# Four graph-attention layers: VectorE reads the row factors G from SBUF instead of from a copy in PSUM

## The chip, the core and the metric

The kernel runs on one core of one Trainium2 chip. The metric is the device time of one execution in microseconds (us). The kernel before took 2712.34 us, the median of three runs (2709.53 to 2713.56).

Engine names as in the profile: PE is TensorE (PEld its weight loads), DVE is VectorE, ACT is ScalarE, POOL is GpSimd, SP is the engine that issues most transfers.

## The reference, cut to what matters

The input `x` has 16 graphs of 1024 nodes with 256 features, all with one 1024 x 1024 adjacency matrix. Four layers follow one another. Each normalises the rows, projects them, forms attention weights over the neighbours, sums the projected rows with them, and adds the result to `x`:

```python
h = jnp.maximum(_layernorm(x, axis=-1), 0.0)
x = x + layer(h, adj, W, a)

# layer, per head (layers 0 and 2 have four heads of 64, layers 1 and 3 one head of 256)
q = h @ W
e = q @ a_src [:, None] + q @ a_dst [None, :]
e = where(e >= 0, e, slope * e)
attn = softmax(where(adj > 0, e, -inf), axis=-1)
out = elu(attn @ q)            # relu in the last layer
```

## The kernel before

The exponential of a leaky sum is the larger of two products, so a tile of unnormalised weights needs no exponential of its own: up to factors that cancel or that are moved into the projected rows, it is `max(G[i], r[j]) * mask[j, i]`, with `G` a row (one value for each target node `i`) and `r` a column (one for each neighbour `j`). VectorE makes such a tile of 128 neighbours by 1024 target nodes in one instruction, TensorE multiplies it with the projected rows, and a column of ones in them gives the denominator.

There are 16 x 4 = 64 steps (graph, layer); half have four heads, half have one. A head has eight weight tiles, so there are 32 x 4 x 8 + 32 x 8 = 1280 in all. The steps of four graphs are interleaved, and the preparation of a step is spread over the aggregation of the steps ahead of it by lists of places (`agenda`).

Preparation of a step, and the pools in which its results lie:

```python
xpool = ...(name="xpool", bufs=STREAMS)                    # STREAMS = 4
ps_g = ...(name="ps_g", bufs=2, space=PSUM)                # G: two banks each
ps_acc = ...(name="ps_acc", bufs=2, space=PSUM)
ps_p = ...(name="ps_p", bufs=2, space=PSUM)

def stats(half):
    for c in range(half * HALF, (half + 1) * HALF):
        nc.vector.bn_stats(bn[:, c, :], xs[b][:, c, :])    # L191
    if half == 1:                                          # L198 to L207
        nc.gpsimd.tensor_tensor(dev, m0, m1, op=ALU.subtract)
        ...                                                # ten short operations on 128 x 8
        nc.gpsimd.tensor_tensor(rstd, rstd, neghalf, op=ALU.pow)        # L204
        ...
        nc.gpsimd.tensor_scalar(shift, shift, -0.5, None, op0=ALU.mult)

def normalise(half):
    for q in range(HALF):
        nc.scalar.activation(xn[:, q, :], xs[b][:, c, :], AF.Identity,  # L213
                             bias=st["shift"][:, c:c + 1], scale=st["rstd"][:, c:c + 1])

def transpose(half, k):
    pt = ps_p.tile([P, HALF, P], F32, name="pp")
    for q in range(HALF):
        nc.tensor.transpose(pt[:, q, :], st["xn", half][:, q, k * P:(k + 1) * P], ident)  # L221
    nc.scalar.activation(st["hT", half][:, k, :], ..., AF.Relu)         # L222

def project(c):
    pw = ps_p.tile([P, F + 2 * H], F32, name="pp")
    ... nc.tensor.matmul(pw, ...)                                       # L233
    ... nc.scalar.activation(whx[:, c, ...], pw[...], ...)              # L235 to L242
    ... nc.gpsimd.tensor_tensor(whx[...], whx[...], ..., op=ALU.mult)   # L244, four heads only
```

`G` goes through device memory to be spread over the partitions. It lands in SBUF (`gs`); ScalarE copies it to PSUM (`g`), and VectorE reads it there:

```python
def fetch(n, h):
    gs = state[n]["gs", h] = work.tile([P, N], F32, name="gs", bufs=2)
    nc.sync.dma_start(out=gs, in_=state[n]["grow"][h]....partition_broadcast(P))

def broadcast(n, h):
    g = state[n]["g", h] = ps_g.tile([P, N], F32, name="g")
    nc.scalar.activation(g, state[n]["gs", h], AF.Copy)                 # L284

def weights(n, h, jc):
    w = state[n]["w", h, jc] = work.tile([P, N], F32, name="w", bufs=WBUFS)   # WBUFS = 18
    nc.vector.scalar_tensor_tensor(w, state[n]["g", h],                 # L289
                                   state[n]["rcol"][:, jc, h:h + 1],
                                   masks[...][:, jc, :], op0=ALU.max, op1=ALU.mult)
```

The mask is a uint8 tile in SBUF. Aggregation and the finish of a step, which runs during the next step:

```python
def aggregate(n, h, i0, per):
    acc = ps_acc.tile([P, per, D + 1], F32, name="acc")
    ... nc.tensor.matmul(acc[...], lhsT=st["w", h, jc][:, o:o + cols],  # L305
                         rhs=st["whx"][:, jc, h, :], start=(jc == 0), stop=(jc == C - 1))
    nc.scalar.activation(st["y"][:, i0:i0 + per, h, :], acc, AF.Copy)   # L309

# finish, in two halves of 128 x 1024
nc.vector.reciprocal(r, y[..., D])                                      # L326
nc.gpsimd.tensor_tensor(yh, yh, r..., op=ALU.mult)                      # L330
nc.gpsimd.tensor_scalar(e, yh, 0.0, -3.0e38, op0=ALU.min, op1=ALU.max)  # L335
nc.scalar.activation(e, e, AF.Exp)                                      # L339
nc.vector.scalar_tensor_tensor(e, e, -1.0, yh, op0=ALU.add, op1=ALU.max)# L345
nc.gpsimd.tensor_add(xh, xh, e)                                         # L346
# last layer, in place of the last four: x = max(y, 0) + x
nc.vector.scalar_tensor_tensor(xh, yh, 0.0, xh, op0=ALU.max, op1=ALU.add)     # L348
```

The order in which VectorE's tiles are emitted is made by `emit_tiles`: a head's copy is emitted when the tiles come within four of it, and the tiles run ahead of TensorE as far as the weight buffers go, which come free a head at a time.

Of the kernel before, what the change touches and what calls it, by code (L numbers as in the profile page):

```python
# [23 lines left out]
F32 = mybir.dt.float32  # L24
# [3 lines left out]
AF = mybir.ActivationFunctionType  # L28
ALU = mybir.AluOpType
AX = mybir.AxisListType  # L30
PSUM = bass.MemoryType.PSUM

P = 128
EPS = 1e-5
SHIFT = 60.0
STREAMS = 4
WBUFS = 18

# [17 lines left out]
def kernel(ctx: ExitStack, tc: tile.TileContext, x, adj, ws, avs, out):  # L58
    nc = tc.nc
    B, N, F = x.shape  # L60
    C = N // P
# [27 lines left out]
    prep = ctx.enter_context(tc.tile_pool(name="prep", bufs=2))  # L89
    small = ctx.enter_context(tc.tile_pool(name="small", bufs=4))  # L90
    work = ctx.enter_context(tc.tile_pool(name="work", bufs=2))
    ps_g = ctx.enter_context(tc.tile_pool(name="ps_g", bufs=2, space=PSUM))
    ps_acc = ctx.enter_context(tc.tile_pool(name="ps_acc", bufs=2, space=PSUM))
    dram = ctx.enter_context(tc.tile_pool(name="dram", bufs=4, space=bass.MemoryType.DRAM))
    ps_p = ctx.enter_context(tc.tile_pool(name="ps_p", bufs=2, space=PSUM))

    L = len(LAYERS)
    steps = order_of_steps(B, L)
# [1 line left out]
    state = [dict() for _ in steps]  # L100
# [48 lines left out]
    def mask_block(jc):  # L149
# [3 lines left out]
        def fetch_block():  # L153
            st["raw"] = work.tile([P, C, P], I32, name="w", bufs=WBUFS)
            nc.scalar.dma_start(out=st["raw"], in_=adj.rearrange("(c p) j -> p c j", p=P)[
                :, :, jc * P:(jc + 1) * P])

        def sign():
            st["sgn"] = work.tile([P, 2, C, P], BF16, name="w", bufs=WBUFS)
            nc.vector.tensor_scalar(st["sgn"][:, 0], st["raw"], -1.0, 1.0, op0=ALU.max,  # L160
                                    op1=ALU.min)
# [17 lines left out]
    def preparation(n):  # L179
# [90 lines left out]


        out += [factors, rows, lambda: fetch_heads(n + 1), lambda: None]
        return [(at, piece) for at, piece in zip(agenda_of[n], out, strict=True)]

    def fetch(n, h):

        gs = state[n]["gs", h] = work.tile([P, N], F32, name="gs", bufs=2)
        nc.sync.dma_start(out=gs, in_=state[n]["grow"][h].rearrange("c i -> (c i)")
                          .partition_broadcast(P))

    def broadcast(n, h):

        g = state[n]["g", h] = ps_g.tile([P, N], F32, name="g")
        nc.scalar.activation(g, state[n]["gs", h], AF.Copy)  # L284

    def weights(n, h, jc):

        w = state[n]["w", h, jc] = work.tile([P, N], F32, name="w", bufs=WBUFS)
        nc.vector.scalar_tensor_tensor(w, state[n]["g", h], state[n]["rcol"][:, jc, h:h + 1],  # L289
                                       masks[LAYERS[steps[n][1]][3]][:, jc, :],  # L290
                                       op0=ALU.max, op1=ALU.mult)

# [72 lines left out]
    def groups(n):  # L365
        if LAYERS[steps[n][1]][0] == 1:
# [3 lines left out]
    tiles = [(n, h, jc) for n, (b, l) in enumerate(steps) for h in range(LAYERS[l][0])  # L370
             for jc in range(C)]
    place = {t: i for i, t in enumerate(tiles)}
    done = {"tiles": 0, "g": 0, "gs": 0, "rows": 0, "free": 0, "prepared": 0}
    agenda = []

    def prepare(upto):

        while agenda and agenda[0][0] <= upto:
            _, n, piece, last = agenda.pop(0)
            piece()  # L380
            if last:
                done["prepared"] = n + 1
# [6 lines left out]
    def fetch_heads(below=0):  # L389

        done["rows"] = max(done["rows"], below)
        while done["gs"] < min(done["g"] + 2 * C, len(tiles)):
            n, h, _ = tiles[done["gs"]]
            if n >= done["rows"]:
                break
            fetch(n, h)
            done["gs"] += C

    def emit_tiles(upto, must=False):
        while done["tiles"] < min(upto, len(tiles)):  # L400
            i = done["tiles"]

            while done["g"] <= min(i + C // 2, len(tiles) - 1):
                n, h, _ = tiles[done["g"]]
                if n >= done["prepared"]:
                    if i < done["g"] or not must:
                        break
                    prepare(max(a[0] for a in agenda if a[1] == n))
                broadcast(n, h)
                done["g"] += C  # L410
                fetch_heads()
            if i >= done["g"]:
                return
            weights(*tiles[i])
            done["tiles"] += 1

    last, agenda_of = {}, []
    for n, (b, l) in enumerate(steps):

        free = 8 * (last[b % STREAMS] + 1) + (8 if l == 0 else 5) if b % STREAMS in last else -99  # L420
# [17 lines left out]
    with tc.manual_schedule():  # L438
# [38 lines left out]
        planned = 2  # L477
        prepare(-2)
        emit_tiles(C, must=True)
        prepare(-1)  # L480
        for i in range(1, STREAMS):
# [7 lines left out]
        for n in range(len(steps)):  # L489
            for k, (h, i0, per) in enumerate(groups(n)):  # L490
                while planned < len(steps) and agenda_of[planned][0] <= 8 * n + k:
                    plan(planned)
                    planned += 1
                emit_tiles(place[n, h, C - 1] + 1, must=True)
                aggregate(n, h, i0, per)
                if i0 + per == C:
                    done["free"] = place[n, h, C - 1] + 1
                while ending and ending[0][0] <= k:
                    ending.pop(0)[1]()
                if 8 * n + k in later:  # L500
                    later[8 * n + k]()
                prepare(8 * n + k)
                ahead = 6 if per > 1 else 3
                emit_tiles(min(done["tiles"] + ahead, done["free"] + WBUFS))
            for _, piece in ending:
                piece()
            ending = finish(n)
# [35 lines left out]
```

## Time and profile before

| what | value |
|---|---|
| time, median of three | 2712.34 us |
| span of the profiled execution | 2711.9 us |
| mean granted TensorE clock | 0.984 |
| TensorE matmul busy | 2567.2 us, 95% |
| VectorE busy | 1900.3 us, 70% |
| ScalarE busy | 1229.6 us, 45% |
| GpSimd busy | 992.3 us, 37% |
| weight tiles on VectorE (L289) | 1280, mean 1273 ns |
| copies of G on ScalarE (L284) | 160, mean 1018 ns, 162.3 us |
| transfers, all queues | 130.12 MB, mean 48 GB/s |

The busy line of the page gives each engine's busy time, its share of the span, and its instructions. The chain that ended last is followed back from the last instruction: each piece is put down to what released it. The groups list instructions of one line with their tiles (out<-in), shape and count, then the busy time, the mean of one, and the idle time just before them with what ended it. In the waits, a line "PE acc L305 <- DVE w L289" is idle time of TensorE that VectorE's writing of w ended. The windows give each engine's busy time in a stretch of the span, and the timeline lists single instructions with start and length.

### The profile page before, as it was taken

How to read it: one execution, taken by the hardware profiler on the slowest of the kernel's cores; microseconds unless marked ns; L12 is line 12 of the kernel's file. 1: busy time of each engine (PE TensorE's matmuls, PEld its weight loads, DVE VectorE, ACT ScalarE, POOL GpSimd, SP SyncE). 2: the span in 40 equal slices, each digit the busy share in tenths (PEclk: the TensorE clock that was granted, in tenths of full speed). 3: DMA queues.
4: the chain of work that ended last, by engine and by line, in shares of the span. 5: the costliest groups of instructions: out<-in, count | busy, mean ns of one | idle time of the engine just before them, and what ended most of it. 6: DMA issues, size and time to landing. Idle time of an engine off the chain costs nothing.

```text
span 2711.9 us, 89498 instructions
## 1 busy us (share of the span) xinstructions
PE 2567.2 (95%) x40080; PEld 2269.2 (84%) x40080; DVE 1900.3 (70%) x2041; ACT 1229.6 (45%) x3337; POOL 992.3 (37%) x1242
## 2 busy tenths in 40 slices
PE   3799999999999999999999999999999999999998
PEld 2688888888888888888888888888888888788876
DVE  3796686477875688666876778748687567678752
ACT  3344445444354554544444454544435444444431
POOL 2133424423424534344242353442332443443321
PEclk9899999999999999999999999999999999999999
DMA  3211011012122011002201211101212110011111
GB/s 117 87 42 45 10 45 41 19 62 66 41 72 71 27 49 41 18 33 72 73 33 49 72 33 42 41 25 57 67 39 72 59 45 18 33 41 42 33 33 55
DMA packets 70846, 130.12 MB, mean 48 GB/s; under 512 B 6208, under 2 KB 49984, under 8 KB 70464
## 3 DMA queue, kind: packets, MB, share of 16 engines
q1 hardware_dynamic: 62144, 120.21, 13.5%
q8 instruction: 316, 5.18, 0.8%
q10 hardware_dynamic: 8320, 4.19, 0.6%
q14 instruction: 66, 0.54, 0.1%
HBM read 106.95 MB, written 17.43 MB: 46 GB/s over the span
## 4 chain that ended last, share of the span: by engine, by line
PE 81%; DVE 8%; ACT 4%; issue 3%; POOL 2%; DMA 1%; ACTq 0%; DVEq 0%; SPq 0%; POOLq 0%
PE acc L305 61%; PE pp L233 16%; DVE w L289 6%; PE pp L221 4%; ACT xn L213 1%; DVE bn L191 1%; DMA w<-in_adj 1%; ACT whx L235 1%; ACT g L284 1%; POOL rstd L204 0%; ACT e L339 0%; POOL y L330 0%; ACT whx L239 0%; PE pp L260 0%; DMA x<-in_x 0%
## 5 line engine op out<-in xcount | busy, mean ns | idle before, releaser
L305 PE MATMUL acc<-whx,w 128*64 128x65 f32 x36864 | 1951.0, 242 | 42.0 <-DVE w L289 28.6
L305 PEld LDWEIGHTS acc<-whx,w 128*64 128x64 f32 x36864 | 1766.8, 145 | 225.2 <-issue 70.4
L289 DVE SCALAR_TENSOR_TENSOR w<-g,rcol,mask 128x1024 f32<-128x1024 f32 x1280 | 1544.1, 1273 | 458.3 <-ACT g L284 412.3
L309 ACT ACTIVATE y<-acc 128x260 f32<-128x260 f32 (+1 forms) x512 | 196.8, 384 | 1085.8 <-PE acc L305 1085.0
L233 PE MATMUL pp<-wx,hT 128*128 128x258 f32 (+1 forms) x2048 | 513.2, 394 | 9.0 <-ACT hT L222 7.6
L330 POOL TENSOR_TENSOR y<-y,r 128x1024 f32<-128x1024 f32 x128 | 242.5, 1899 | 594.9 <-DVE r L326 594.9
L233 PEld LDWEIGHTS pp<-wx,hT 128*128 128x128 f32 x2048 | 375.1, 191 | 79.6 <-ACT hT L222 9.9
L346 POOL TENSOR_TENSOR x<-x,e 128x1024 f32<-128x1024 f32 x96 | 226.7, 2366 | 278.0 <-DVE e L345 264.2
L244 POOL TENSOR_TENSOR whx<-whx 128x256 f32<-128x256 f32 x256 | 159.9, 630 | 444.9 <-ACT whx L242 443.5
L213 ACT ACTIVATE xn<-x,shift,rstd 128x256 f32<-128x256 f32 x512 | 264.1, 590 | 126.3 <-POOL shift L207 126.0
L345 DVE SCALAR_TENSOR_TENSOR e<-e,y 128x1024 f32<-128x1024 f32 x96 | 117.6, 1225 | 197.0 <-ACT e L339 197.0
L235 ACT ACTIVATE whx<-pp,nbias 128x4 f32<-128x4 f32 (+1 forms) x512 | 135.0, 264 | 163.1 <-PE pp L233 151.8
L221 PE MATMUL pp<-ident,xn 128*128 128x128 f32 x1024 | 158.0, 287 | 39.0 <-ACT xn L213 28.3
L191 DVE BATCH_NORM_STATS2 bn<-x 128x6 f32<-128x256 f32 x512 | 172.9, 407 | 16.9 <-DMA x<-in_x 14.2
L221 PEld LDWEIGHTS pp<-ident,xn 128*128 128x128 f32 x1024 | 117.3, 144 | 76.7 <-ACT xn L213 36.3
L284 ACT ACTIVATE g<-gs 128x1024 f32<-128x1024 f32 x160 | 162.3, 1018 | 5.3 <-DVE w L289 5.3
L222 ACT ACTIVATE hT<-pp 128x512 f32<-128x512 f32 x256 | 143.2, 592 | 18.5 <-PE pp L221 16.5
L198 POOL TENSOR_TENSOR dev<-bn 128x8 f32<-128x8 f32 x64 | 16.4, 256 | 290.7 <-DVE bn L191 290.7
L239 ACT ACTIVATE whx<-pp,whx 128x256 f32<-128x256 f32 x256 | 121.7, 475 | 0.0
L339 ACT ACTIVATE e<-e 128x1024 f32<-128x1024 f32 x96 | 100.8, 1050 | 33.1 <-POOL e L335 33.1
L204 POOL TENSOR_TENSOR rstd<-rstd,neghalf 128x8 f32<-128x8 f32 x64 | 106.7, 1668 | 5.0
L335 POOL TENSOR_SCALAR e<-y 128x1024 f32<-128x1024 f32 x96 | 100.0, 1042 | 8.5
(45 smaller groups left out, 553.8 us busy)
## 6 DMA issues: line engine op xcount, KB each, us to landing
gs<-grow SPq DMA_DIRECT2D x160, 512.0 KB
x<-in_x SPq DMA_DIRECT2D x16, 1024.0 KB
out<-x SPq DMA_DIRECT2D x32, 512.0 KB
w<-in_adj ACTq DMA_DIRECT2D x8, 512.0 KB
wx<-in_L_gnn_W SPq DMA_DIRECT2D x4, 256.0 KB
e<-in_L_gnn_a SPq DMA_DIRECT2D x8, 128.0 KB
grow<-gT SPq DMA_DIRECT2D x32, 16.0 KB
grow<-gT SPq DMA_DIRECT2D x32, 4.0 KB
```

The source lines that it names most:

```text
L191: nc.vector.bn_stats(bn[:, c, :], xs[b][:, c, :])
L213: nc.scalar.activation(xn[:, q, :], xs[b][:, c, :], AF.Identity, bias=st["shift"][:, c:c + 1], scale=st["rstd"][:, c:c + 1])
L221: nc.tensor.transpose(pt[:, q, :], st["xn", half][:, q, k * P:(k + 1) * P], ident)
L233: nc.tensor.matmul(pw, lhsT=st["hT", half][:, k, q * P:(q + 1) * P], rhs=wx[l][:, k, :], start=(k == 0), stop=(k == K - 1))
L235: nc.scalar.activation(whx[:, c, :, D], pw[:, F + H:F + 2 * H], AF.Exp, bias=nbias[l], scale=slope)
L244: nc.gpsimd.tensor_tensor(whx[:, c, :, 0:D], whx[:, c, :, 0:D], whx[:, c, :, D:D + 1].to_broadcast([P, H, D]), op=ALU.mult)
L284: nc.scalar.activation(g, state[n]["gs", h], AF.Copy)
L289: nc.vector.scalar_tensor_tensor(w, state[n]["g", h], state[n]["rcol"][:, jc, h:h + 1], masks[LAYERS[steps[n][1]][3]][:, jc, :], op0=ALU.m ...
L305: nc.tensor.matmul(acc[o % P:o % P + cols, q, :], lhsT=st["w", h, jc][:, o:o + cols], rhs=st["whx"][:, jc, h, :], start=(jc == 0), stop=(j ...
L309: nc.scalar.activation(st["y"][:, i0:i0 + per, h, :], acc, AF.Copy)
L330: nc.gpsimd.tensor_tensor(yh, yh, r[:, :, None].to_broadcast([P, HALF * H, D]), op=ALU.mult)
L346: nc.gpsimd.tensor_add(xh, xh, e)
```

## The change

VectorE reads `gs` in SBUF, where the transfer lands it. ScalarE's copy and the PSUM tile `g` go, and with them the condition that a tile waits for its copy to have been emitted. Two G tiles took four of the eight banks of PSUM: these go to two more accumulators and two more buffers for transposes and projections. `gs` is now held until the last of the eight tiles of a head has read it, so it has three buffers in place of two, and the weight tiles have 17 in place of 18, which keeps the use of SBUF the same. The purpose is to take work off ScalarE, to cut a hop out of the way of G, and to give TensorE more room in PSUM.

```diff
-WBUFS = 18
+GBUFS = 3
+WBUFS = 17
...
-    ps_g = ctx.enter_context(tc.tile_pool(name="ps_g", bufs=2, space=PSUM))
-    ps_acc = ctx.enter_context(tc.tile_pool(name="ps_acc", bufs=2, space=PSUM))
+    ps_acc = ctx.enter_context(tc.tile_pool(name="ps_acc", bufs=4, space=PSUM))
...
-    ps_p = ctx.enter_context(tc.tile_pool(name="ps_p", bufs=2, space=PSUM))
+    ps_p = ctx.enter_context(tc.tile_pool(name="ps_p", bufs=4, space=PSUM))
...
-        gs = state[n]["gs", h] = work.tile([P, N], F32, name="gs", bufs=2)
+        gs = state[n]["gs", h] = work.tile([P, N], F32, name="gs", bufs=GBUFS)
...
-    def broadcast(n, h):
-
-        g = state[n]["g", h] = ps_g.tile([P, N], F32, name="g")
-        nc.scalar.activation(g, state[n]["gs", h], AF.Copy)
...
-        nc.vector.scalar_tensor_tensor(w, state[n]["g", h], state[n]["rcol"][:, jc, h:h + 1],
+        nc.vector.scalar_tensor_tensor(w, state[n]["gs", h], state[n]["rcol"][:, jc, h:h + 1],
...
-        while done["gs"] < min(done["g"] + 2 * C, len(tiles)):
+        while done["gs"] < min((done["tiles"] // C + GBUFS) * C, len(tiles)):
...
-            i = done["tiles"]
-
-            while done["g"] <= min(i + C // 2, len(tiles) - 1):
-                n, h, _ = tiles[done["g"]]
+            n, h, jc = tiles[done["tiles"]]
+            if jc == 0:
                 if n >= done["prepared"]:
-                    if i < done["g"] or not must:
-                        break
+                    if not must:
+                        return
                     prepare(max(a[0] for a in agenda if a[1] == n))
-                broadcast(n, h)
-                done["g"] += C
                 fetch_heads()
-            if i >= done["g"]:
-                return
-            weights(*tiles[i])
+            weights(n, h, jc)
             done["tiles"] += 1
```

More of the change, by code (lines that the diff above doesn't have):

```diff
@@ L372 @@
     place = {t: i for i, t in enumerate(tiles)}
-    done = {"tiles": 0, "g": 0, "gs": 0, "rows": 0, "free": 0, "prepared": 0}
+    done = {"tiles": 0, "gs": 0, "rows": 0, "free": 0, "prepared": 0}
     agenda = []
```

## The prediction

> **What bounds the kernel now.** I read the page's busy line first, then the groups of GpSimd, then the waits of TensorE, then the timeline around GpSimd's short operations.
>
> ```profile
> PE 2567.2 (95%) x40080; PEld 2269.2 (84%) x40080; DVE 1900.3 (70%) x2041; ACT 1229.6 (45%) x3337; POOL 992.3 (37%) x1242
> ...
> PE acc L305 61%; PE pp L233 16%; DVE w L289 6%; PE pp L221 4%; ACT xn L213 1%; DVE bn L191 1%; DMA w<-in_adj 1%; ACT whx L235 1%; ACT g L284 1%; POOL rstd L204 0%; ACT e L339 0%; POOL y L330 0%; ACT whx L239 0%; PE pp L260 0%; DMA x<-in_x 0%
> ```
>
> TensorE is busy for 2567 of 2712 us, and three of its lines (L305, L233, L221) make 81% of the chain that ended last. Only 2712 - 2567 = 145 us of its time is open to any change that leaves its work alone, and the windows put 57 us of that in the first 100 us, ahead of the steady part. The other lines of the chain are no queues of their own: they are places where TensorE had to wait. Its waits say for what:
>
> ```profile
> PE pp L137 <- DVE sq L131: 29.4, 3, 24.7
> PE acc L305 <- DVE w L289: 28.6, 40, 1.5
> PE pp L221 <- ACT xn L213: 28.3, 29, 8.9
> ```
>
> The columns are total us, times, longest. The first is the start. The second says that VectorE's weight tiles are late 40 times, by at most 1.5 us. The third says that 29 times in 64 steps the transposes stand ready before the normalised rows: **that chain has hardly any slack now**. The large wait of VectorE on the copy (w on g, 412 us in 54 times) costs little by itself, because VectorE is ahead of TensorE when it happens.
>
> GpSimd's groups, in the same notation as the page (busy us, mean ns):
>
> ```profile
> L330 POOL TENSOR_TENSOR y<-y,r 128x1024 f32<-128x1024 f32 x128 | 242.5, 1899 | 594.9 <-DVE r L326 594.9
> L346 POOL TENSOR_TENSOR x<-x,e 128x1024 f32<-128x1024 f32 x96 | 226.7, 2366 | 278.0 <-DVE e L345 264.2 <-PE acc L305 13.6 <-issue 0.2
> L244 POOL TENSOR_TENSOR whx<-whx 128x256 f32<-128x256 f32 x256 | 159.9, 630 | 444.9 <-ACT whx L242 443.5
> L204 POOL TENSOR_TENSOR rstd<-rstd,neghalf 128x8 f32<-128x8 f32 x64 | 106.7, 1668 | 5.0
> L335 POOL TENSOR_SCALAR e<-y 128x1024 f32<-128x1024 f32 x96 | 100.0, 1042 | 8.5
> ```
>
> [...] VectorE's L345 and L348 have two SBUF inputs. Here is GpSimd's chain of short statistics (first fence) beside VectorE (second; start us, length us):
>
> ```profile
> 742.92 1.24 POOL L202 TENSOR_SCALAR rstd<-rstd 128x8 f32<-128x8 f32 x1
> 744.25 0.21 POOL L203 TENSOR_TENSOR rstd<-rstd,dev 128x8 f32<-128x8 f32 x1
> 744.53 1.67 POOL L204 TENSOR_TENSOR rstd<-rstd,neghalf 128x8 f32<-128x8 f32 x1
> 746.17 0.21 POOL L205 TENSOR_TENSOR shift<-bn 128x8 f32<-128x8 f32 x1
> 746.45 1.27 POOL L206 TENSOR_TENSOR shift<-shift,rstd 128x8 f32<-128x8 f32 x1
> ```
>
> ```profile
> 742.85 1.23 DVE L345 SCALAR_TENSOR_TENSOR e<-e,y 128x1024 f32<-128x1024 f32 x1 [6.95 <-ACT e L339]
> 746.44 1.23 DVE L345 SCALAR_TENSOR_TENSOR e<-e,y 128x1024 f32<-128x1024 f32 x1 [2.36 <-ACT e L339]
> ```
>
> L202 and L206 take 0.23 and 0.21 us at the median; the two that begin with an L345 take 1.24 and 1.27, ending where it ends. L204 lies free. The other way round:
>
> ```profile
> L348 DVE SCALAR_TENSOR_TENSOR x<-y,x x32: 1206/1215/2897, 578.7 to 2706.3; 128x1024 f32<-128x1024 f32 x32
> L289 DVE SCALAR_TENSOR_TENSOR w<-g,rcol,mask x1280: 1181/1274/1286, 78.2 to 2674.4; 128x1024 f32<-128x1024 f32 x183
> ```
>
> (min/median/max ns.) The L348 that begins at 853.64 us, while an L330 is running, loses 2897 - 1206 = 1.69 us. L289, with g in PSUM and only the mask in SBUF, never exceeds 1.29 us in 1280 instructions, whatever GpSimd does.
>
> [...] The trace gives 1273 ns (L289 mean) against 1225 (L345 mean), 48 ns; I use the trace. [...] TensorE's wait for an accumulator (L305 on y L309) is 0.9 us in all.
>
> **The change part by part.** TensorE's and GpSimd's instruction order is unchanged; ScalarE loses its copies, and VectorE's order moves by a tile here and there.
>
> *Removed:* 160 ScalarE copies at 1018 ns, 162 us. ScalarE is busy for 45%, so almost all of it lies beside other work. *Moved:* the 1280 weight tiles read 48 ns faster: 61 us of VectorE, of which TensorE can get back at most its 28.6 us of waits on w. *Four projection buffers:* TensorE waits for whx to be read about 8 us in all. *Four accumulators:* 0.9 us, though they will also let ScalarE run late. *One weight buffer less, one G buffer more:* VectorE can be 9 tiles ahead of a head in use, before 10; a tile is 1.2 us, small. All gains together: at most 40 us.
>
> *Added, and the crux:* the 1280 instructions now have two SBUF inputs, gs and mask, and enter the exclusion with GpSimd. **First, throughput.** [...] The L330 held L348 back for 1.69 us and had begun about 0.08 us earlier (two of them end at 851.71 + 3.75 us), so about 0.13 us less than its length. By that: L330 1.77 x 128 = 226 us, L346 2.24 x 96 = 215, L244 0.50 x 256 = 128, L335 0.91 x 96 = 87, nine short ones in each of 64 preparations at 0.08 = 46: 702 us, 71% of GpSimd's busy time. [...]
>
> Now eight steps of the steady state, from 1008.5 to 1331.6 us: 323 us, VectorE 231.5, GpSimd 123.4. They have 160 tiles, so 231.5 - 160 x 0.048 + 0.71 x 123.4 = 311 us: VectorE with all of GpSimd's holds in its way just fits, at 96%. But it isn't even, and 17 weight buffers can't carry work from one step to the next beyond a head. The same sum step by step exceeds the step's length in three: the four-head step 1008.5 to 1054.5 (43.1 - 1.5 + 14.1 = 55.7 for 46.0), and two one-head steps (1054.5 to 1087.0 and 1250.8 to 1283.3) by some 0.5 and 2. That is 12 us in eight steps, 96 us in 64.
>
> **Second, latency.** Statistics to shift are ten short GpSimd operations one after another, 4.2 us alone (nine of about 0.21 on 0.29 us centres, and the 1.67 of L204). With VectorE running tiles back to back, each one [...] waits about 1.15 us: ten waits make some 12 us, 8 more than now. The finish of a step (two L330, two L335, two L346) waits likewise. Then come the rows' normalisation and TensorE's transposes, in fixed order: xn on ScalarE ends its first half at 748.09 + 2.07 = 750.16 us and the transposes begin at 751.83, a slack of 1.7 us; 29 times it was none. I take a slack of 4 us on the average, so a stall of 4 us, in three quarters of the 64 steps (in one-head steps VectorE fills its buffers, stops, and leaves GpSimd alone): 4 x 48 = 192 us. The 4 and the three quarters are my choice.
>
> Sum: 192 + half of 96 (while TensorE waits for xn, VectorE catches up) - 40 = +200 us: **2910 us**, 7% slower.
>
> **Rivals.** *No contention with a uint8 mask, or only a little:* then only the gains stand, 2670 to 2700 us, and TensorE is busy for 96%. For it: no instruction of exactly this form is in the trace. Against it: L345, L348 and even L124 (in the start) show it whenever two inputs lie in SBUF. *VectorE, back to back, starves GpSimd:* preparation waits until VectorE's buffers are full, and the stalls double: 3050 to 3150. Against it: at 855.41 us L198 is held for 1.19 us by one L348, ends, and L199 is held by the next, so GpSimd gets in between two. *Transfers of G become the wait:* 160 x 512 KB is unchanged, 3 buffers instead of 2, each held for eight tiles (10 us) instead of one copy; DMA moves 48 GB/s on the mean. I give it under 20 us. *The holds hide:* VectorE is idle for 30%, and if the holds fall into idle time the loss is 80 us, 2790.
>
> **Range and chances.** The low end, 2790, is the hidden case; the high end, 3070, has every step's chain stalled by 5 to 6 us. Mean and sign rest on an exclusion seen in both directions, the size on a slack that I estimated. Faster by over 2% needs more than 54 us out of gains that I bound by 40.
>
> **What would show it.** Right: the weight tiles (w, then at L284) have a minimum near 1.21 us but a mean of 1.5 to 1.7, and maxima over 3 us; GpSimd's short operations go from 0.21 to about 1.1 us, and its busy time rises above 1300 us; TensorE's wait for xn rises from 28 to over 150 us, that for w to over 50; ScalarE's busy time falls by 162 us. Wrong: w at 1.22 us throughout with GpSimd unchanged (no contention), or waits on gs by DMA in VectorE's list.

## The result, and the profile after

The changed kernel takes 2830.36 us (median of 4 runs, 2828.66 to 2832.53) against 2712.92 us before: a ratio of 1.0436, 95% interval 1.0418 to 1.0454. It is 117 us slower. 2910 was forecast, with a range from 2790 to 3070.

From the page of the changed kernel, the busy line and the chain that ended last by line:

```profile
PE 2603.5 (92%) x40080; PEld 2314.6 (82%) x40080; DVE 2246.0 (79%) x2041; ACT 1070.0 (38%) x3177; POOL 1528.6 (54%) x1242
...
PE acc L300 45%; DVE w L284 13%; PE pp L233 13%; PE pp L221 4%; POOL rstd L204 2%; DVE bn L191 2%; DMA gs<-grow 1%; POOL y L325 1%; ACT xn L213 1%; POOL dev L198 1%; POOL dev L199 1%; POOL rstd L202 1%; POOL rstd L201 1%; POOL dev L200 1%; POOL rstd L203 1%
```

ScalarE lost its 160 us. VectorE and GpSimd, whose instructions are as many as before, are busy for 346 and 536 us more. In the chain, w went from 6 to 13%, and the short statistics of GpSimd (dev, rstd) have come in. The time itself parts into two: TensorE's idle time went from 145 to 2831 - 2604 = 227 us, 82 more, and its busy time rose by 36.

TensorE's waits in the changed kernel (total us, times, longest):

```profile
PE pp L221 <- ACT xn L213: 81.0, 17, 15.2
PE acc L300 <- DVE w L284: 56.9, 51, 7.1
PE pp L137 <- DVE sq L131: 28.6, 2, 24.3
PE pp L260 <- ACT gcol L255: 18.8, 7, 4.9
```

The first two are the two that the prediction named, and their longest went from 8.9 to 15.2 and from 1.5 to 7.1 us. GpSimd's groups (busy us, mean ns):

```profile
L244 POOL TENSOR_TENSOR whx<-whx 128x256 f32<-128x256 f32 x256 | 307.5, 1213 | 340.4 <-ACT whx L242 339.5
L341 POOL TENSOR_TENSOR x<-x,e 128x1024 f32<-128x1024 f32 x96 | 297.0, 3100 | 162.5 <-DVE e L340 162.3
L325 POOL TENSOR_TENSOR y<-y,r 128x1024 f32<-128x1024 f32 x128 | 279.2, 2185 | 448.2 <-DVE r L321 448.1
```

The scaling of the projected rows doubled, from 630 to 1213 ns; the sum into x went from 2366 to 3100. How that comes about is seen in one place of the timeline, GpSimd first, then VectorE (start us, length us):

```profile
1074.22 1.17 POOL L198 TENSOR_TENSOR dev<-bn 128x8 f32<-128x8 f32 x1 [16.94 <-DVE bn L191]
1075.47 1.11 POOL L199 TENSOR_TENSOR dev<-dev 128x8 f32<-128x8 f32 x1
1076.67 1.10 POOL L200 TENSOR_SCALAR dev<-dev 128x8 f32<-128x8 f32 x1
1077.84 1.14 POOL L201 TENSOR_TENSOR rstd<-bn 128x8 f32<-128x8 f32 x1
...
1086.41 1.14 POOL L207 TENSOR_SCALAR shift<-shift 128x8 f32<-128x8 f32 x1
1087.52 2.89 POOL L325 TENSOR_TENSOR y<-y,r 128x1024 f32<-128x1024 f32 x1
1090.50 1.89 POOL L330 TENSOR_SCALAR e<-y 128x1024 f32<-128x1024 f32 x1
```

```profile
1074.06 10.83 DVE L284 SCALAR_TENSOR_TENSOR w<-gs,rcol,mask 128x1024 f32<-128x1024 f32 x9
...
1085.08 8.39 DVE L284 SCALAR_TENSOR_TENSOR w<-gs,rcol,mask 128x1024 f32<-128x1024 f32 x5
```

A run of tiles in the kernel before, for the spacing:

```profile
700.78 9.61 DVE L289 SCALAR_TENSOR_TENSOR w<-g,rcol,mask 128x1024 f32<-128x1024 f32 x8
```

One short operation of GpSimd gets in per tile of VectorE, on 1.2 us centres; the ten of them take from 1074.2 to 1087.6, 13.3 us for 4.2 alone. VectorE pays nothing for them: nine tiles in 10.83 us are (10.83 - 1.27) / 8 = 1.195 us from start to start, and it was (9.61 - 1.27) / 7 = 1.191 in the kernel before. It pays for the two large ones that follow (L325 and L330): five tiles in 8.39 us, in place of some 6.1, and each large one lengthens one tile (to 2.92 and 2.05 us). ScalarE stands still for 13.09 us in this place, waiting for `shift`.

All weight tiles by their durations (min/median/max ns), from the line's own view:

```profile
L284 DVE SCALAR_TENSOR_TENSOR w<-gs,rcol,mask x1280: 1176/1274/3399, 60.3 to 2792.8; 128x1024 f32<-128x1024 f32 x183
```

The maximum went from 1286 to 3399 ns, the median stayed at 1274.

### The profile page after: what moved, and what is told of

It is laid out like the page before. It is cut to its first block, busy times and chain, and to the rows that moved or that the text cites. A ratio compares the mean times of both kernels' runs of the same rounds, so it can differ in the third digit from the quotient of the medians.

```text
span 2830.7 us, 89051 instructions
## 1 busy us (share of the span) xinstructions
PE 2603.5 (92%) x40080; PEld 2314.6 (82%) x40080; DVE 2246.0 (79%) x2041; ACT 1070.0 (38%) x3177; POOL 1528.6 (54%) x1242
## 4 chain that ended last, share of the span: by engine, by line
PE 61%; DVE 15%; POOL 11%; issue 6%; DMA 3%; ACT 3%; ACTq 0%; DVEq 0%; SPq 0%; POOLq 0%
PE acc L300 45%; DVE w L284 13%; PE pp L233 13%; PE pp L221 4%; POOL rstd L204 2%; DVE bn L191 2%; DMA gs<-grow 1%; POOL y L325 1%; ACT xn L213 1%; POOL dev L198 1%; POOL dev L199 1%; POOL rstd L202 1%; POOL rstd L201 1%; POOL dev L200 1%; POOL rstd L203 1%
## 5 line engine op out<-in xcount | busy, mean ns | idle before, releaser
L300 PE MATMUL acc<-whx,w 128*64 128x65 f32 x36864 | 1985.4, 245 | 70.1 <-DVE w L284 56.9
L300 PEld LDWEIGHTS acc<-whx,w 128*64 128x64 f32 x36864 | 1798.2, 148 | 257.5 <-DVE w L284 70.9
L284 DVE SCALAR_TENSOR_TENSOR w<-gs,rcol,mask 128x1024 f32<-128x1024 f32 x1280 | 1860.9, 1518 | 127.9 <-DMA gs<-grow 69.7
L325 POOL TENSOR_TENSOR y<-y,r 128x1024 f32<-128x1024 f32 x128 | 279.2, 2185 | 448.2 <-DVE r L321 448.1
L244 POOL TENSOR_TENSOR whx<-whx 128x256 f32<-128x256 f32 x256 | 307.5, 1213 | 340.4 <-ACT whx L242 339.5
L213 ACT ACTIVATE xn<-x,shift,rstd 128x256 f32<-128x256 f32 x512 | 264.1, 590 | 324.9 <-POOL shift L207 324.6
L341 POOL TENSOR_TENSOR x<-x,e 128x1024 f32<-128x1024 f32 x96 | 297.0, 3100 | 162.5 <-DVE e L340 162.3
L340 DVE SCALAR_TENSOR_TENSOR e<-e,y 128x1024 f32<-128x1024 f32 x96 | 143.4, 1494 | 231.8 <-ACT e L334 231.8
L221 PE MATMUL pp<-ident,xn 128*128 128x128 f32 x1024 | 162.2, 297 | 86.7 <-ACT xn L213 81.0
L221 PEld LDWEIGHTS pp<-ident,xn 128*128 128x128 f32 x1024 | 126.9, 150 | 116.0 <-ACT xn L213 96.4
L198 POOL TENSOR_TENSOR dev<-bn 128x8 f32<-128x8 f32 x64 | 44.3, 693 | 256.5 <-DVE bn L191 256.5
L204 POOL TENSOR_TENSOR rstd<-rstd,neghalf 128x8 f32<-128x8 f32 x64 | 135.2, 2113 | 5.0
L330 POOL TENSOR_SCALAR e<-y 128x1024 f32<-128x1024 f32 x96 | 129.6, 1350 | 8.5
```

What stands on the lines that cost most here:

```text
L244: nc.gpsimd.tensor_tensor(whx[:, c, :, 0:D], whx[:, c, :, 0:D], whx[:, c, :, D:D + 1].to_broadcast([P, H, D]), op=ALU.mult)
L284: nc.vector.scalar_tensor_tensor(w, state[n]["gs", h], state[n]["rcol"][:, jc, h:h + 1], masks[LAYERS[steps[n][1]][3]][:, jc, :], op0=ALU. ...
L300: nc.tensor.matmul(acc[o % P:o % P + cols, q, :], lhsT=st["w", h, jc][:, o:o + cols], rhs=st["whx"][:, jc, h, :], start=(jc == 0), stop=(j ...
L325: nc.gpsimd.tensor_tensor(yh, yh, r[:, :, None].to_broadcast([P, HALF * H, D]), op=ALU.mult)
```

## The experiments

The theory, from the trace of before: an instruction of VectorE with two SBUF inputs and an operation of GpSimd hold each other up (an L202 beside an L345 took 1.24 us in place of 0.23, an L348 beside an L330 took 2.90 in place of 1.21). I call that the exclusion. With gs in SBUF each weight tile has two SBUF inputs, which costs in two ways, the **holds** of VectorE by large operations, and the **latency** of the short chain in front of the transposes. The rivals: the order of emission, the one weight buffer less, and the PSUM banks with what they let ScalarE do. All ratios are against the kernel before, run on the same chip.

### The read alone, and the rest without it

e1: the kernel before, with one operand changed (and the buffers of SBUF as in the change):

```diff
-        nc.vector.scalar_tensor_tensor(w, state[n]["g", h], ...
+        nc.vector.scalar_tensor_tensor(w, state[n]["gs", h], ...
```

> The kernel before, with its copy of G to PSUM, its banks and its order of emission all kept; VectorE alone reads gs in place of g (17 weight buffers and 3 of gs, as in the change, so that gs can be held). Exclusion between VectorE's two SBUF inputs and GpSimd: the whole loss comes with this one operand, 2800 to 2860 us, weight tiles at a mean of 1.45 to 1.6 us with some over 3 us, GpSimd busy over 1400 us. Rival, the order of emission and the banks of PSUM cost the time: within 20 us of 2713.

2902.81 us, ratio 1.0701 (1.0685 to 1.0718). The operand alone costs 190 us, more than the whole change, with tiles at a mean of 1517 ns (1273 before). So the rest of the change gives 72 us back. e1 lies above the 2800 to 2860 us that I had expected of it.

e2: the weight buffers.

```diff
-WBUFS = 18
+WBUFS = 17
```

> The kernel before with 17 weight buffers in place of 18, nothing else. Exclusion: 2705 to 2725 us, the one buffer is worth next to nothing. Rival, the lost buffer is what holds VectorE back: 2760 us or more.

2711.10 us, ratio 0.9992 (0.9983 to 1.0001): the buffer is worth nothing that can be measured.

### What the rest gives back

e3, the changed kernel with both PSUM pools at two buffers; e10, with two accumulators and four projection buffers:

```diff
# e3                              # e10
-name="ps_acc", bufs=4            -name="ps_acc", bufs=4
+name="ps_acc", bufs=2            +name="ps_acc", bufs=2
-name="ps_p", bufs=4
+name="ps_p", bufs=2
```

> The changed kernel with two accumulators and two projection buffers again (four banks of PSUM left empty). Exclusion: 2825 to 2850 us, the banks are worth less than 20 us. Rival, the deeper PSUM lets ScalarE run late and does the harm: below 2780 us. Rival, the deeper PSUM hides much of a larger loss: above 2870 us.

> The changed kernel with two accumulators and its four projection buffers. The deeper PSUM is worth 63 us (e3 against the changed kernel). TensorE's waits in e3 name the reading of whx (L239, L242) and not the eviction of accumulators, so if these waits are the whole of it: 2825 to 2850 us. If the four accumulators carry it, because ScalarE stands at xn and evicts late: 2870 to 2895.

e3: 2893.26 us, ratio 1.0659 (1.0641 to 1.0677). e10: 2829.47 us, ratio 1.0439 (1.0421 to 1.0456), as much as the changed kernel. The two projection buffers are worth 64 us, the two accumulators nothing. e3's waits of TensorE on projection buffers (the lines with whx) say why:

```profile
PE pp L221 <- ACT xn L213: 82.2, 22, 15.2
...
PE pp L233 <- ACT whx L239: 13.5, 6, 2.4
PE pp L221 <- ACT whx L239: 13.3, 17, 2.4
```

A wait of pp on whx is TensorE standing at a projection buffer that ScalarE has not read yet. In the kernel before, the same kind of wait is 0.5 us at its longest. In e3 all four lines of this kind make 49.3 us, in the changed kernel 4.9. In the place shown above, ScalarE starts nothing else in the 13.09 us that it stands at xn. In all it stands there for longer than before, first e3, then before:

```profile
ACT xn L213 <- POOL shift L207: 320.0, 47, 19.1
ACT xn L213 <- POOL shift L207: 126.0, 52, 6.8
```

In the changed kernel it stands there as long (324.6 us), but with four buffers TensorE goes on. That is the last of the three outcomes told for e3: the deeper PSUM hides a part of a larger loss. Since e1 and e3 differ by the copy and the order alone, those two are worth 2903 - 2893 = 10 us.

### Half of the tiles without the exclusion

e4: the changed kernel with two and two buffers in PSUM, and the masks of the first four neighbour blocks left in the four free banks. They are the transposed signs themselves, which are the mask as long as adj has no negative entry.

```diff
+    pmask = [maskp.tile([P, C, P], BF16, name=f"pmask{jc}") for jc in range(HALF)]
...
-            pm = st["pm"] = ps_acc.tile([P, C, P], BF16, name="acc")
+            pm = st["pm"] = pmask[jc] if jc < HALF else ps_acc.tile(...)
...
-                                       masks[LAYERS[steps[n][1]][3]][:, jc, :],
+                                       pmask[jc] if jc < HALF else masks[...][:, jc, :],
```

> The changed kernel with two accumulators and two projection buffers, and the masks of the first four of the eight neighbour blocks kept in the four free banks of PSUM (the transposed signs themselves, which equal both masks as long as adj has no negative entry). Half of the tiles then have one SBUF input. Exclusion: those tiles never exceed 1.3 us and the loss against before falls to a half or less, 2735 to 2785 us. Rival, reading G from SBUF costs by itself, or the order does: about 2830 us.

2694.72 us, ratio 0.9927 (0.9912 to 0.9941): faster than both kernels, and 199 us faster than e3, from which it differs in the place of half of the masks, and in that these four need no preparation at the start: the first aggregation begins at 79.3 us, at 89.8 in e3. That is 10 of the 199 us (before, it began at 85.3). The tiles by the mask that they read:

```profile
L288 DVE SCALAR_TENSOR_TENSOR w<-gs,rcol,pmask x640: 1231/1273/1282, 57.9 to 2650.2; 128x1024 f32<-128x1024 f32 x160
L288 DVE SCALAR_TENSOR_TENSOR w<-gs,rcol,mask x640: 1179/1276/3378, 62.6 to 2655.0; 128x1024 f32<-128x1024 f32 x160
```

Same source gs, same engine: with the mask in PSUM none of 640 exceeds 1282 ns, with the mask in SBUF they reach 3378. It is the second SBUF input that matters, not where G lies. I had expected 2735 to 2785, a half or less of the loss; the whole of it went. So with half of the tiles open to holds, what they lose does not show in the time: the 640 tiles with the mask in SBUF have a mean of 1435 ns, the others 1273, some 104 us of VectorE in all.

e4 also answers a sign that I had named for being wrong, and that came: in the changed kernel VectorE waits on the transfers of G.

```profile
DVE w L284 <- DMA gs<-grow: 69.7, 23, 23.0
```

In e4 the same wait is 71.2 us in 24 times, and the loss is gone. It stands where the wait on ScalarE's copy stood before (412 us), and is not what costs the time.

e11, every second block, with the masks in SBUF cut to the other four and the room given to weight buffers (against e4):

```diff
-WBUFS = 17
+WBUFS = 19
...
-    masks = [const.tile([P, C, N], U8, name=f"mask{i}") for i in range(2)]
+    masks = [const.tile([P, HALF, N], U8, name=f"mask{i}") for i in range(2)]
...
-            pm = st["pm"] = pmask[jc] if jc < HALF else ps_acc.tile(...)
+            pm = st["pm"] = (ps_acc.tile(...) if jc % 2
+                             else pmask[jc // 2])
```

> As e4, but every second neighbour block has its mask in PSUM in place of the first four, and the SBUF that this frees goes to weight buffers (19 in place of 17). [...] 2675 to 2695 us, a little below e4's 2695. If a run of four free tiles is what lets GpSimd work undisturbed, alternation is worse: 2700 to 2730.

2698.86 us, ratio 0.9952 (0.9936 to 0.9969): no better than e4, against my expectation of 2675 to 2695. TensorE waits less for w (24.0 us against 37.7) and more for xn (32.2 against 23.2).

### Holds against latency

e7, e8 and e9 cut GpSimd's large operations to 8 columns (the scaling of whx, the division, the minimum and the sum into x are left out but for these, and the exponential is a relu) and keep its short ones; e7 is that cut in the kernel before, e8 in the changed one, e9 in e1.

```diff
-                nc.gpsimd.tensor_tensor(whx[:, c, :, 0:D], whx[:, c, :, 0:D], ...
+                nc.gpsimd.tensor_tensor(whx[:, c, 0, 0:8], whx[:, c, 0, 0:8], ...
-            nc.gpsimd.tensor_tensor(yh, yh, r[:, :, None]..., op=ALU.mult)
+            nc.gpsimd.tensor_tensor(yh[:, 0, 0:8], yh[:, 0, 0:8], r[:, 0:1]..., op=ALU.mult)
-                nc.gpsimd.tensor_scalar(e, yh, 0.0, -3.0e38, ...)
+                nc.gpsimd.tensor_scalar(e[:, 0, 0:8], yh[:, 0, 0:8], 0.0, -3.0e38, ...)
-                nc.scalar.activation(e, e, AF.Exp)
+                nc.scalar.activation(e, yh, AF.Relu)
-                nc.gpsimd.tensor_add(xh, xh, e)
+                nc.gpsimd.tensor_scalar(xh[:, 0, 0:8], e[:, 0, 0:8], 0.0, None, op0=ALU.mult)
```

> The kernel before with GpSimd's large operations cut to 8 columns (the scaling of the projected rows, the division, the minimum and the sum into x are left out but for these columns; the exponential is a relu of y). The short statistics stay. 2680 to 2715 us: GpSimd is not in the way there.

> The same cut in the changed kernel. Exclusion: without large holds no weight tile exceeds 1.5 us, and what is left of the loss against the same cut of before is the latency of the short operations: 30 to 70 us above e7. If the loss lay mainly in VectorE's throughput: within 20 us of e7. Rival without exclusion (order, buffers, banks): still about 118 us above e7.

> The read alone (as e1: banks, copy and order of before, VectorE reads gs), with GpSimd's large operations cut to 8 columns as in e7 and e8 (the same parts are left out). It parts the two ways in which the exclusion costs, without the deeper PSUM that can hide them: what is left above e7 (2703 us) is the latency of the short operations; the rest of e1's 190 us is the large holds. As I predicted it (latency two thirds, holds one third): 2800 to 2850. If the holds are the larger part: 2710 to 2780.

e7: 2702.86 us (ratio 0.9967, 0.9954 to 0.9980). e8: 2702.92 (0.9961, 0.9946 to 0.9976). e9: 2780.61 (1.0248, 1.0231 to 1.0265). With two and two buffers in PSUM, then, the short operations alone cost 2781 - 2703 = 78 us. That is at the edge of what I had told for the holds as the larger part (2710 to 2780), and under the 2800 to 2850 of my prediction's shares. TensorE's wait for weight tiles is 23.5 us in e9 and 33.6 in e7, so it is not on them that the time is lost. The cost shows in front of the transposes: the wait for xn was 25.4 us in e7, that of L221 for whx on L242 4.7. e9's waits of TensorE:

```profile
PE pp L221 <- ACT xn L213: 64.3, 16, 15.2
PE pp L137 <- DVE sq L131: 30.5, 2, 23.4
PE acc L305 <- DVE w L289: 23.5, 21, 5.8
PE pp L221 <- ACT whx L242: 19.5, 23, 3.1
```

What is left of the 190 us, 112, went with the large operations. e8 has the same latency (its wait for xn is 64.0 us) and no loss, against my expectation of 30 to 70: the rest of the change gives back 78 us there, about as much as it gives back in full, 72. So e8 alone would have said that the latency costs nothing; only e9, without the deeper PSUM, parts them. In the changed kernel as it stands the whole loss goes with the large operations, 2830 us with them and 2703 without.

The 112 us are not all shown to be holds of VectorE. The cut also removes the large operations' own delays (L244 went from 630 to 1213 ns), and may let the short chain begin earlier: of TensorE's waits in the changed kernel that for w falls from 56.9 to 26.8 us in e8, that for xn from 81.0 to 64.0. No run parts these, and the two terms need not add up exactly.

### Taking the short chain off GpSimd

e5 (in the changed kernel) and e6 (in the kernel before) do the statistics on VectorE in seven operations, with the power alone left on GpSimd:

```diff
-                nc.gpsimd.tensor_tensor(dev, m0, m1, op=ALU.subtract)
-                ...                                   # nine of the ten
+                nc.vector.tensor_tensor(dev, m0, m1, op=ALU.subtract)
+                ...                                   # seven, two pairs joined
                 nc.gpsimd.tensor_tensor(rstd, rstd, neghalf, op=ALU.pow)
```

> The changed kernel with nine of GpSimd's ten short statistics operations on VectorE (as seven), only the power left on GpSimd. If the latency of that chain (about 11 us where VectorE is full, against 4.2 alone) is the larger part of the loss: TensorE's wait for xn falls from 81 to under 40 us and the time to 2760 to 2790 us. If the time is lost mainly to the large operations' holds on VectorE: at most 20 us better, 2810 to 2830.

> The same move in the kernel before. The chain is 4.2 us there and seldom held, so 2690 to 2715 us; a version better than before would be one that lies under 2705. If the short operations on VectorE lengthen its queue where four-head steps need tiles: up to 2730.

e5: 2837.81 us, ratio 1.0460 (1.0444 to 1.0475). e6: 2754.26, ratio 1.0154 (1.0137 to 1.0171); neither a gain, and both above every range that I had told for them. For the theory e5 is inconclusive, since it takes one wait away and makes another. Its waits of TensorE, and one of VectorE:

```profile
PE acc L300 <- DVE w L284: 149.2, 131, 11.7
...
PE pp L221 <- ACT xn L213: 15.9, 8, 7.4
```

```profile
DVE shift L206 <- POOL rstd L204: 132.1, 64, 10.0
```

The wait for xn fell from 81.0 to 15.9, as expected; but VectorE now stands 64 times in its own queue for the power, 132 us, with the weight tiles behind it, and that for w rose from 56.9 to 149.2.

### Why a tile is not faster from SBUF

e12: a constant in place of the column factor (the factor is left out of the result).

```diff
-        nc.vector.scalar_tensor_tensor(w, state[n]["gs", h], state[n]["rcol"][:, jc, h:h + 1],
+        nc.vector.scalar_tensor_tensor(w, state[n]["gs", h], 1.0,
```

> The changed kernel with the constant 1.0 in place of the column factor rcol in the weight tiles (the factor is left out of the result). Held by nobody, a tile takes 1274 ns and starts 1196 ns after the one before, from SBUF as from PSUM (1191), against 1224 for L340, which has a constant there. If reading the column factor is what costs the 50 ns: the tiles that are not held take 1220 to 1230. If the uint8 mask costs it: 1274 as before. Time within 2% of the changed kernel in both.

The line of the weight tiles (min/median/max):

```profile
L284 DVE SCALAR_TENSOR_TENSOR w<-gs,mask x1280: 1152/1214/3390, 59.8 to 2797.1; 128x1024 f32<-128x1024 f32 x183
```

1214 in place of 1274: reading the column factor costs 60 ns. The uint8 mask costs nothing that shows: the tile is then no longer than L345 of the kernel before, which has a constant and two float32 inputs (median 1225). The time, of a single run, is 2837.31 us, no gain from tiles 60 ns shorter.

## Why the prediction was right, and where its terms were off

**Direction and cause: right.** The exclusion was read, in both directions, from the few instructions of the trace of before that already had two SBUF inputs: L345, L348, and L124, beside which an L205 took 0.51 us in place of 0.21. It doesn't come with every pair there: three times an L345 begins just after an L204, and the L204 takes 1.67 us, the mean of its line, and the L345 1.25, 0.03 over its median. e1 and e4 show the exclusion to be the cause: the operand alone makes the loss, and moving half of the other operand out of SBUF takes it away. None of the rivals made the loss: the weight buffer is worth nothing (e2), order and copies give 10 us back, the transfers of G are waited for as long in e4, which has no loss, and GpSimd is not starved: in the place shown it gets in after each tile, on 1.2 us centres.

**The size, term by term:**

| term | predicted us | measured us | from |
|---|---|---|---|
| latency of the short chain | +192 | +78 | e9 - e7 |
| holds on VectorE | +48 | +112, with all else that the large operations cost | e1's 190 less 78 |
| gains of all other parts | -40 at most | -72 | the change - e1 |
| of which projection buffers | -8 | -64 | e10 - e3 |
| sum | +200 | +118 | |

The measured terms close to 118 because two of them are differences. That 2910 came as near as 80 us is in part luck: a latency 114 us too large covered large operations 64 us too small, and gains 32 us too small added to it.

*Latency.* The course was as told: ten operations were to take about 12 us, and take 13.3 in the place shown. The term failed in what I called my choice, 4 us in 48 steps, and of the two in the 48. In many steps the chain lies where VectorE is not full: by its starts and ends in the trace it takes 8.6 us on the mean (4.7 before), and over 11 us in 14 of the 64 steps. TensorE's matmuls wait for xn 17 times in the changed kernel, 4.8 us on the mean, not 48 times.

*Holds.* The working by steps hits the step that it singled out: 55.7 us was worked out for the four-head step at 1008.5 us, and it takes 56.2. (Two smaller errors offset one another there: VectorE is busy for some 12 us more than before, where 14.1 were reckoned, and the 1.5 us of faster tiles did not come.) Its windows before and after (stretch, length, busy PE, PEld, DVE, ACT, POOL, clock, DMA share, GB/s), with a four-head step that the working left alone:

```profile
1008.50:1054.50 46.00, 41.87 (x1062) 38.10 (x1057) 43.13 (x38) 19.29 (x54) 19.83 (x24) 1.00 0.04 15
1202.90:1250.80 47.90, 46.29 (x1096) 41.59 (x1095) 37.98 (x34) 21.51 (x66) 11.90 (x19) 1.00 0.20 58
```

```profile
1073.80:1130.00 56.20, 47.41 (x1061) 42.51 (x1056) 55.43 (x39) 16.56 (x51) 40.22 (x24) 0.91 0.06 22
1277.60:1324.50 46.90, 46.45 (x1096) 41.76 (x1095) 43.77 (x33) 18.31 (x64) 25.21 (x19) 1.00 0.18 59
```

VectorE fills the first step wholly and the second not. Over the whole run its busy time rose by 346 us, half of the 702 us of holds that I had worked out for the case that all of them meet a tile. What failed is the way from eight steps to 64, and the halving of the result: the steps of the first 450 us, where four-head steps follow one another and VectorE was busy throughout in two of them even before, weren't in the sample. These two of before (each from the end of the last step's last eviction to that of its own), 143.7 to 185.0 us and 354.7 to 402.6, became 148.8 to 208.8 and 390.6 to 450.8 us, 19 and 12 us longer. At the end of the second, the run is 48 of its 118 us behind.

*Gains.* I bounded the projection buffers by TensorE's waits in the trace of before, 8 us, where ScalarE stood at xn for 126 us. The change itself makes ScalarE late (324.6 us), and then they are worth 64. I had written that four accumulators would let ScalarE run late and had given it no number; of the two pools it was the other one that carried it (e10).

*Faster tiles.* The 61 us of VectorE's time for an SBUF source were not there at all. The medians are 1274 ns with G in PSUM and 1274 with G in SBUF. The 48 ns that I had read between L289 and L345 are the column factor's (60 ns by e12), not the source's. As the term was capped by TensorE's waits on w anyway, it moved the sum little.

*The signs in the profile.* The mean of 1.5 to 1.7 us for a tile (1518), maxima over 3 us (3399), GpSimd over 1300 us (1529), the wait for w over 50 us (56.9), ScalarE 160 us less: as told. The wait for xn, told at over 150 us, is 81. The short operations reach 1.1 us in places such as the one shown; six of the ten keep a median of 0.2. The minimum of a tile, told at 1.21 us, is 1.176, as before (1.181), and the median did not move.

## What to carry to other kernels

Before an operand is moved from PSUM to SBUF, count the SBUF inputs that the VectorE instruction has afterwards, and look in the trace at a GpSimd operation that begins beside an instruction which already has two: a copy that looks idle may be what keeps the two engines apart. Here the copy took 162 us of ScalarE, and reading the operand in SBUF cost 190 us (e1). To get rid of the copy, move the other operand to PSUM, and it need not be all of it: half of the masks was enough to be 0.7% faster than before. And the worth of a buffer is not its wait in the trace of before, if the same change delays the engine that empties it (8 us by the trace, 64 measured).

## What the runs showed that I had not expected

- In the place shown, short GpSimd operations get in between two weight tiles at no cost to VectorE (1.195 us from tile to tile, 1.191 in the kernel before), while nine of the ten take 0.96 to 1.29 us, for 0.20 to 0.24 alone.
- The column factor read per partition costs a VectorE tile of 128 x 1024 60 ns (1274 against 1214 with a constant); G from SBUF or from PSUM (medians 1274 and 1274), and a mask in uint8 from SBUF or in bf16 from PSUM (1276 and 1273 in e4), make no difference where a tile is not held.
- In the changed kernel TensorE's granted clock is lower where it stalls. It is 0.961 on the mean against 0.984, and in the step shown above 0.91 against 1.00, with TensorE busy for 47.4 us with the 41.9 us of work of before. In the step that has no stall it is 1.00, and the busy time is the same. Over the whole run TensorE's busy time is 36 us longer, 30% of the loss. That the stalls cause the lower clock wasn't tested by itself, nor that the clock makes the 36 us: in e8 it is 0.975, under the 0.984 of before, and the time is 2702.92 us, shorter than the 2712.92 of before.
